# Roots as powers on GpSimd, and an adjacency scaled once, in a four-layer graph network

## The chip, the cores and the metric

The kernel runs on one core of a Trainium2 chip. The metric is the device time of one execution in microseconds (us). A core has five engines with a queue each: PE (TensorE, matrix products), DVE (VectorE), ACT (ScalarE), POOL (GpSimd) and SP (SyncE, which here only issues DMAs). Each engine takes its instructions strictly in the order in which the program holds them; an instruction whose input is late holds up everything behind it on that engine.

## The reference, cut to what matters

64 graphs of 256 nodes with 128 features, with a symmetric 0/1 adjacency each, go through four layers. Each layer adds its result to its input and normalizes every node.

```python
def _layernorm(x, eps=1e-5):
    return (x - mean(x)) / sqrt(var(x) + eps)

x = _layernorm(x + layer0(x, adj))   # max over neighbours of relu(p_i + q_j + b)
x = _layernorm(x + layer1(x, adj))   # elu products, two aggregations, tanh
x = _layernorm(x + layer2(x, adj))   # below
x = _layernorm(x + layer3(x, adj))   # sum over neighbours of gelu(layernorm(c_j + d_i)), an update, a layernorm of its own

def layer2(x, adj):
    A = adj + eye(256)
    deg = A.sum(-1)
    dinv = where(deg > 0, rsqrt(deg), 0)
    norm_A = dinv[:, None] * A * dinv[None, :]
    h = elu(elu(x @ W0 + b0))
    h = elu(norm_A @ (h @ W1) + b1)
    return norm_A @ (h @ W2) + b2
```

## The kernel before

There are two programs in the kernel. One, `sparse`, runs always; the other, `general`, stands behind a branch that is taken only if the adjacency doesn't have the expected shape, and with these inputs it is not taken. Both use the class `Shared`, which holds the layers.

In `sparse` the work of one graph is cut into four stages, each a Python generator: `first` (layer 0 and the sorting of neighbours into slots, L502), `second` (layer 1, L778), `third` (layer 2 and the start of layer 3, L782) and `last` (the rest of layer 3, L821). All 64 graphs are unrolled. At each step four graphs are in work, one in each stage (L881): `together` (L341) lets the generator that has come least far, by weights of 34, 34, 14 and 44, issue instructions up to its next `yield`. That gives an order of issue; a scheduler of the framework then makes of it the order on each engine, by readiness of the instructions and by the free buffers of the pools. So a removed instruction can also move others.

The parts that matter here:

- `inverse_root(t)` (L72) is an ACT square root in place (L74) and a DVE reciprocal in place (L75). It serves the norms (`rs`, 128x2, one column for each half of the nodes), the degrees of layer 2 (`dinv`, 128x2) and the per-message roots of layer 3 (`vr`, 128x16 or 108x16, L768).
- ACT's functions come in tables. Square root, Exp (and Tanh) and Gelu have tables of their own here, and each change between them puts a table load in front of the activation. A load carries the line of the activation behind it.
- `layernorm` (L166) takes the statistics of each half (L171, L172), writes variance plus epsilon to `rs` (L174), calls `inverse_root` between two `yield`s, and then normalizes (L180, or L184 and L185 with a gain and a shift). Each graph has five such norms: x after layers 0, 1 and 2, and z and o in `update` (L319).
- `layer_2` (L261) computes the degrees' root, adds the identity to the transposed adjacency `aT` (L277), and then twice scales the rows of `hs` by `dinv` (L293, four instructions of 128x128 per graph), multiplies by `aT` on PE (L296), copies (L299), multiplies by the weights (L304), and scales by `dinv` and adds the bias (L308).
- The degree sums `dg` are made in `first` (L544) and kept until `third`, which turns them into `deg` (L787).
- In `sums_of` and `last`, layer 3 is done in tiles of 1024 messages: PE gathers (L728), DVE adds (L732), ACT squares (L736), PE sums over the features (L743), ACT adds epsilon (L745), a trip through DRAM gives the roots a compact form (L750, L762, `vr`, L771) and spreads them over all partitions (L828), DVE multiplies (L839), ACT applies Gelu (L841), DVE adds up (L492).

Of the kernel before, what the change touches and what calls it, by code (L numbers as in the profile page):

```python
# [9 lines left out]
F32 = mybir.dt.float32  # L10
BF16 = mybir.dt.bfloat16
AF = mybir.ActivationFunctionType
ALU = mybir.AluOpType
# [6 lines left out]
P = 128  # L20
# [23 lines left out]
def kernel(  # L44
# [9 lines left out]
    nc = tc.nc  # L54
    B, N, D = x.shape
    assert N == 2 * P and D == P
    H = N // P
    Q = P // 4

    consts = ctx.enter_context(tc.tile_pool(name="consts", bufs=1))  # L60
# [8 lines left out]
    minus1 = consts.tile([P, 1], F32, name="minus1")  # L69
    nc.vector.memset(minus1, -1.0)  # L70

    def inverse_root(t):  # L72

        nc.scalar.activation(t, t, AF.Sqrt)  # L74
        nc.vector.reciprocal(t, t)  # L75

    def load(src, shape, name):
        t = consts.tile(shape, F32, name=name)
# [43 lines left out]
    with tc.tile_pool(name="prep", bufs=1) as prep, tc.tile_pool(  # L122
        name="ps_prep", bufs=2, space=bass.MemoryType.PSUM
# [33 lines left out]
    class Shared:  # L157
# [45 lines left out]
        def to_features(self, xn, name, bufs=None):  # L203
# [5 lines left out]
            nc.scalar.copy(t, pt[:, :N])  # L209
            return t  # L210

        def node_tile(self, name):
            return self.state.tile([P, H, P], F32, name=name)

# [43 lines left out]
            yield from self.layernorm(x2, y)  # L258
            s["x2"] = x2

        def layer_2(self, s, aT, deg_of):  # L261

            work, psum, elu = self.work, self.psum, self.elu
            x2 = s["x2"]
            deg = work.tile([P, H], F32, name="deg")
            deg_of(deg)
            nc.vector.tensor_scalar(deg, deg, 1.0, None, ALU.add)
            pos = work.tile([P, H], F32, name="pos")
            nc.vector.tensor_scalar(pos, deg, 0.0, None, ALU.is_gt)
            dinv = work.tile([P, H], F32, name="dinv")  # L270
            nc.vector.tensor_scalar(dinv, deg, 1e-30, None, ALU.max)
            inverse_root(dinv)
            yield
            nc.vector.tensor_mul(dinv, dinv, pos)
            for h in range(H):
                blk = aT[:, h, h * P:(h + 1) * P]
                nc.vector.tensor_add(blk, blk, ident)  # L277
            yield
            xT = self.to_features(x2, "xT_2", 1)
            yield  # L280
            ph = psum()
            hs = work.tile([P, H, P], F32, name="hs")
            for h in range(H):
                cols = slice(h * P, (h + 1) * P)
                nc.tensor.matmul(ph[:, cols], xT[:, cols], w2[0], start=True, stop=True)
            yield
            for h in range(H):
                nc.vector.tensor_add(hs[:, h], ph[:, h * P:(h + 1) * P], b2[0])
            yield from elu(hs, hs, twice=True)
            yield  # L290
            for step in (1, 2):
                for h in range(H):
                    nc.vector.tensor_scalar(hs[:, h], hs[:, h], dinv[:, h:h + 1], None, ALU.mult)  # L293
                pa = psum()
                for h in range(H):
                    nc.tensor.matmul(pa[:, :N], hs[:, h], aT[:, h], start=h == 0, stop=h == H - 1)  # L296
                yield
                agg = work.tile([P, N], F32, name="agg")
                nc.scalar.copy(agg, pa[:, :N])  # L299
                yield  # L300
                po = psum()
                for h in range(H):
                    cols = slice(h * P, (h + 1) * P)
                    nc.tensor.matmul(po[:, cols], agg[:, cols], w2[step], start=True, stop=True)  # L304
                yield
                hs = work.tile([P, H, P], F32, name="hs")
                for h in range(H):
                    nc.vector.scalar_tensor_tensor(  # L308
                        hs[:, h], po[:, h * P:(h + 1) * P], dinv[:, h:h + 1], b2[step], ALU.mult, ALU.add
                    )  # L310
                if step == 1:
                    yield from elu(hs, hs)
                yield
            nc.vector.tensor_add(hs, hs, x2)
            x3 = self.node_tile("x3")
            yield from self.layernorm(x3, hs)
            s["x3"] = x3
# [36 lines left out]
    def sparse(ctx):  # L354
# [35 lines left out]
        with tc.tile_pool(name="cs_prep", bufs=1) as pp:  # L390
            t = pp.tile([P, P], F32, name="upto_f")
# [4 lines left out]
            t = pp.tile([P, N], I32, name="iota_i")  # L396
            nc.gpsimd.iota(t, pattern=[[1, N]], base=0, channel_multiplier=0)
            nc.vector.tensor_copy(iota_k, t)
            t = pp.tile([P, 1], I32, name="part_i")
# [25 lines left out]
            t = pp.tile([P, 1], F32, name="gbe")  # L425
# [9 lines left out]
            for i in range(3):  # L435
                t = pp.tile([3, P], BF16, name="u_part")
# [5 lines left out]
            t = pp.tile([ROWS, g_n, g_w], F32, name="tail_f")  # L442
# [7 lines left out]
        state = ctx.enter_context(tc.tile_pool(name="state", bufs=2))  # L450
# [4 lines left out]
        sh = Shared(work, state, ps_mm)  # L455
# [46 lines left out]
        def first(g, s):  # L502
# [37 lines left out]
            nc.scalar.activation(diff, diff, AF.Abs, accum_out=fl[:, 0:1])  # L540
            kc = work.tile([P, H, H], F32, name="kc")
            nc.vector.scalar_tensor_tensor(kc, pc, -1.0, down_c, ALU.mult, ALU.subtract)
            dg = state.tile([P, H], F32, name="dg", bufs=3)
            nc.vector.tensor_reduce(dg, pc, AX.X, ALU.add)  # L544
            s["dg"] = dg

            more = work.tile([P, H, H], F32, name="more")
            for h in range(H):
# [169 lines left out]
        def sums_of(s, i):  # L718
# [46 lines left out]
                fu[:rows],  # L765
                s["fulls"].rearrange("h w -> (h w)")[first_at:first_at + n].rearrange("(p k) -> p k", k=PIECE),
            )
            inverse_root(vr[:rows])  # L768
            nc.vector.tensor_mul(vr[:rows], vr[:rows], fu[:rows])
            out_line = dram.tile([1, GROUP * TILE], F32, name="scale_line")  # L770
            nc.sync.dma_start(out_line[:, :n].rearrange("o (p k) -> (o p) k", k=PIECE), vr[:rows])  # L771
# [9 lines left out]

        def third(g, s):  # L782

            dg = s["dg"]

            def deg_of(deg):
                nc.vector.tensor_scalar(deg, dg, 1.0 / N, None, ALU.mult)  # L787

            yield from sh.layer_2(s, s["aT"], deg_of)
            yield  # L790
            x3, perm = s["x3"], s["perm"]

            x3T = sh.to_features(x3, "x3T")
            yield
            pc = psum()
            for h in range(H):
                nc.tensor.matmul(
                    pc[:, h * N:(h + 1) * N], x3T[:, h * P:(h + 1) * P], w3c.rearrange("p c o -> p (c o)"),
                    start=True, stop=True,
                )  # L800
            pcv = pc.rearrange("p (h c o) -> p h c o", h=H, c=2)
            dn = work.tile([P, H, P], F32, name="dn")
            nc.scalar.copy(dn, pcv[:, :, 1])
            c3 = state.tile([P, 3, H, P], BF16, name="c3")
            split3(c3, pcv[:, :, 0])
            yield
            pd = psum()
            for h in range(H):
                for hi in range(H):
                    nc.tensor.matmul(  # L810
                        pd[:, h * N:(h + 1) * N], dn[:, hi], perm[:, h, hi], start=hi == 0, stop=hi == H - 1
                    )
            yield
            dT = state.tile([P, H, N], F32, name="dT")
            nc.scalar.activation(dT, pd.rearrange("p (h n) -> p h n", h=H), AF.Identity, bias=b3c)
            s.update(x3T=x3T, c3=c3, dT=dT)
            yield
            for i in range(AHEAD):
                yield from sums_of(s, i)
# [75 lines left out]
    def general(ctx):  # L895
# [82 lines left out]
        def middle(g, s):  # L978
# [7 lines left out]
                nc.scalar.copy(aT[:, hj], pt[:, :N])  # L986
            yield

            def deg_of(deg):
                nc.vector.tensor_reduce(deg, an, AX.X, ALU.add)  # L990

            yield from sh.layer_1(s, an, aT, s["x1"])
            yield
            yield from sh.layer_2(s, aT, deg_of)
            yield

            x3T = sh.to_features(s["x3"], "x3T")
# [145 lines left out]
```

## Time and profile before

| what | value |
|---|---|
| median of 3 runs | 5735.95 us (5717.65 to 5736.4) |
| the profiled execution's own time | 5731.62 us |
| its span, first to last instruction | 5729.7 us |
| mean granted TensorE clock | 0.862 |
| table loads on ACT | 1,236, 1.283 us each |
| DMA, mean busy share of 16 engines | about 20%, 64 GB/s |

The profile describes one execution. Its page gives the busy time of each engine, the chain of work that ended last (followed back from the last instruction, at each step to what released it or to the instruction before it on its engine), and groups of instructions. A group's line reads: source line, engine, operation, output and input tiles with their shapes, number, then the busy time in us and the mean ns of one, then the idle time of the engine just before them and what ended it. A line of the waits gives who waited for whom, the total in us, how many times, and the longest. The sum of busy times can count overlapping ends twice: the next instruction on DVE starts some 0.08 us before the one ahead of it is recorded as ended.

### The profile page before, as it was taken

How to read it: one execution, taken by the hardware profiler on the slowest of the kernel's cores; microseconds unless marked ns; L12 is line 12 of the kernel's file. 1: busy time of each engine (PE TensorE's matmuls, PEld its weight loads, DVE VectorE, ACT ScalarE, POOL GpSimd, SP SyncE). 2: the span in 40 equal slices, each digit the busy share in tenths (PEclk: the TensorE clock that was granted, in tenths of full speed). 3: DMA queues.
4: the chain of work that ended last, by engine and by line, in shares of the span. 5: the costliest groups of instructions: out<-in, count | busy, mean ns of one | idle time of the engine just before them, and what ended most of it. 6: DMA issues, size and time to landing. Idle time of an engine off the chain costs nothing.

```text
span 5729.7 us, 83531 instructions
## 1 busy us (share of the span) xinstructions
PE 4529.9 (79%) x27408; PEld 2508.7 (44%) x27408; DVE 4834.4 (84%) x14654; ACT 4275.2 (75%) x6485; POOL 1.9 (0%) x10
## 2 busy tenths in 40 slices
PE   5878878878778778788788788787887887877875
PEld 2444444444444444444444444444444444444443
DVE  6788888888888888888888888888888888888876
ACT  2577777777777777777777777777777777777785
POOL 0000000000000000000000000000000000000000
PEclk8888889889889889888898898898888887888986
DMA  0122222222212221221221222122212212221222
GB/s 22 44 70 63 62 63 72 62 63 66 69 57 70 65 63 63 72 63 62 63 72 62 63 65 70 59 68 65 63 62 72 64 62 63 69 66 60 68 65 74
DMA packets 292813, 365.15 MB, mean 64 GB/s; under 512 B 151952, under 2 KB 210448, under 8 KB 292368
## 3 DMA queue, kind: packets, MB, share of 16 engines
q1 hardware_dynamic: 292368, 359.73, 20.0%
q8 instruction: 217, 3.56, 0.3%
q14 instruction: 228, 1.87, 0.1%
HBM read 345.07 MB, written 14.53 MB: 63 GB/s over the span
## 4 chain that ended last, share of the span: by engine, by line
PE 52%; DVE 29%; ACT 11%; issue 4%; DMA 3%; SPq 0%; DVEq 0%; POOL 0%; ACTq 0%
PE bigp L665 11%; PE bigp L728 8%; DVE pre L839 6%; PE mm L860 5%; DVE lanes L492 4%; PE mm L743 4%; DVE hot L629 4%; DVE pre L732 4%; DVE sums L492 3%; PE bigp L681 3%; DMA rs_s<-scale_line 2%; PE mm L870 2%; PE mm L296 2%; PE mm L699 2%; PE mm L647 2%
## 5 line engine op out<-in xcount | busy, mean ns | idle before, releaser
L665 PE MATMUL bigp<-hot,q 128*128 128x512 fp8e4 (+1 forms) x3840 | 1052.3, 371 | 66.6 <-DVE lanes L492 52.6
L728 PE MATMUL bigp<-hot,c 128*128 128x512 fp8e4 (+1 forms) x3840 | 928.8, 372 | 140.2 <-DVE pre L732 140.2
L732 DVE TENSOR_TENSOR pre<-bigp,dT 128x512 f32<-128x512 f32 (+6 forms) x1664 | 846.3, 530 | 37.8 <-PE bigp L728 33.5
L492 DVE TENSOR_TENSOR lanes<-bigp,lanes 128x512 f32<-128x512 f32 (+6 forms) x1536 | 772.7, 503 | 94.6 <-PE bigp L681 86.9
L839 DVE TENSOR_TENSOR pre<-pre,rs_s 128x1024 f32<-128x1024 f32 (+1 forms) x640 | 732.9, 1150 | 48.6 <-DMA rs_s<-scale_line 48.0
L736 ACT ACTIVATE sq<-pre 128x1024 f32<-128x1024 f32 (+1 forms) x640 | 638.5, 998 | 169.9 <-DVE pre L732 163.9
L841 ACT ACT_TABLE_LOAD x535 | 686.4, 1283 | 9.5
L492 DVE TENSOR_TENSOR sums<-pre,sums 128x1024 f32<-128x1024 f32 (+6 forms) x1024 | 628.8, 614 | 41.2 <-ACT pre L841 40.7
L745 ACT ACTIVATE row<-mm,eps_t 128x256 f32<-128x256 f32 (+1 forms) x640 | 289.6, 453 | 476.9 <-PE mm L743 476.7
L841 ACT ACTIVATE pre<-pre,be,g 128x1024 f32<-128x1024 f32 (+1 forms) x512 | 594.2, 1172 | 57.8 <-DVE pre L839 53.0
L743 PE MATMUL mm<-sq,ones 128*32 128x256 f32 (+1 forms) x5120 | 482.9, 440 | 135.2 <-ACT sq L736 135.2
L74 ACT ACT_TABLE_LOAD x445 | 570.9, 1283 | 7.5
L728 PEld LDWEIGHTS <-c 128*128 128x128 bf16 x3840 | 331.2, 98 | 550.5 <-issue 136.1
L665 PEld LDWEIGHTS <-q 128*128 128x128 bf16 x3840 | 310.8, 97 | 392.6 <-issue 112.0
L296 PE MATMUL mm<-aT,hs 128*128 128x256 f32 x512 | 232.3, 600 | 316.1 <-DVE hs L293 214.8
L629 DVE TENSOR_SCALAR hot<-rank 128x512 fp8e4<-128x512 bf16 (+5 forms) x1536 | 440.5, 348 | 0.0
L681 PEld LDWEIGHTS <-pick 42*128 42x128 bf16 x2944 | 155.8, 95 | 481.5 <-issue 474.2
L296 PEld LDWEIGHTS mm<-aT,hs 128*128 128x128 f32 x512 | 135.6, 293 | 425.8 <-issue 316.1
L860 PE MATMUL mm<-w3u,sums 128*128 128x128 f32 x2048 | 296.7, 289 | 18.4 <-DVE sums L492 16.1
L194 ACT ACT_TABLE_LOAD x221 | 283.5, 1283 | 3.9
L681 PE MATMUL bigp<-lack,pick 42*128 42x36 bf16 (+16 forms) x2944 | 285.7, 187 | 0.0
L860 PEld LDWEIGHTS mm<-w3u,sums 128*128 128x128 f32 x2048 | 254.5, 195 | 37.3 <-issue 17.6
(226 smaller groups left out, 7132.6 us busy)
## 6 DMA issues: line engine op xcount, KB each, us to landing
rs_s<-scale_line SPq DMA_DIRECT2D x512, 512.0 KB
rs_s<-scale_line SPq DMA_DIRECT2D x128, 352.0 KB
an<-in_adj SPq DMA_DIRECT2D x64, 256.0 KB
x<-in_x SPq DMA_DIRECT2D x64, 128.0 KB
line<-row SPq DMA_DIRECT2D x512, 4.0 KB
out<-o SPq DMA_DIRECT2D x64, 128.0 KB
fu<-fulls SPq DMA_DIRECT2D x192, 4.0 KB
vr<-line SPq DMA_DIRECT2D x192, 8.0 KB
```

What stands on the lines that cost most here:

```text
L74: nc.scalar.activation(t, t, AF.Sqrt)
L492: nc.vector.tensor_tensor(lanes[:, :k, :w], src[:, i:i + k], lanes[:, :k, :w], op)
L629: nc.vector.tensor_scalar(hot[:, :, at:at + w], rank[:, :, :w], s0 + i + 1.0 - FAR, None, ALU.is_equal, saturate=False)
L665: nc.tensor.matmul(pt[:, :tl], q3[:, i, h], hot[:, h, t0:t0 + tl], start=i == 0, stop=False)
L681: nc.tensor.matmul(o_, l_, r_, start=False, stop=i == len(todo) - 1)
L728: nc.tensor.matmul(pt[:, :bl], c3[:, k, h], hot[:, h, t0 + b:t0 + b + bl], start=k == 0, stop=k == 2)
L732: nc.vector.tensor_add(block(pre[:, b:], n, w, at), block(pt, n, w, at), widen(dT[:, h, :w], n))
L736: nc.scalar.activation(sq[:, :tl], pre[:, :tl], AF.Square)
L743: nc.tensor.matmul(pr[q * Q:(q + 1) * Q, :tl // 4], ones[:, :Q], v4[:, :, q], start=True, stop=True)
L839: nc.vector.tensor_mul(pre[:, :tl], pre[:, :tl], rs[:, :tl])
L841: nc.scalar.activation(msg[:, :tl], pre[:, :tl], AF.Gelu, bias=be3, scale=g3)
L860: nc.tensor.matmul(pt[:, cols], lanes[:, k, cols], w3u[:, 1], start=k == 0, stop=False)
```

## The change

`inverse_root` becomes one GpSimd instruction that raises the tile to the power of a constant tile of -0.5. The roots of `vr` keep the square root on ACT and the reciprocal on DVE, now written out at their place. The degrees' root is computed in `first`, right after the degree sums, and held for `third`; its product with `pos` goes to GpSimd too. In `layer_2` the transposed adjacency is multiplied once by `dinv` (two instructions of 128x256 per graph), and the scalings of `hs` are gone. The weights of the stages stay.

```diff
+    mhalf = consts.tile([P, 16], F32, name="mhalf")
+    nc.vector.memset(mhalf, -0.5)
...
     def inverse_root(t):
-        nc.scalar.activation(t, t, AF.Sqrt)
-        nc.vector.reciprocal(t, t)
+        nc.gpsimd.tensor_tensor(t, t, mhalf[:t.shape[0], :t.free_size()], ALU.pow)
...
+        def inverse_root_of(self, deg, bufs):
+            nc.vector.tensor_scalar(deg, deg, 1.0, None, ALU.add)
+            pos = self.work.tile([P, H], F32, name="pos")
+            nc.vector.tensor_scalar(pos, deg, 0.0, None, ALU.is_gt)
+            dinv = self.state.tile([P, H], F32, name="dinv", bufs=bufs)
+            nc.vector.tensor_scalar(dinv, deg, 1e-30, None, ALU.max)
+            inverse_root(dinv)
+            nc.gpsimd.tensor_mul(dinv, dinv, pos)
+            return dinv
...
-        def layer_2(self, s, aT, deg_of):
+        def layer_2(self, s, aT, dinv_of):
...
+            dinv = dinv_of()
+            yield
             for h in range(H):
                 blk = aT[:, h, h * P:(h + 1) * P]
                 nc.vector.tensor_add(blk, blk, ident)
+            for h in range(H):
+                nc.vector.tensor_scalar(aT[:, h], aT[:, h], dinv[:, h:h + 1], None, ALU.mult)
...
             for step in (1, 2):
-                for h in range(H):
-                    nc.vector.tensor_scalar(hs[:, h], hs[:, h], dinv[:, h:h + 1], None, ALU.mult)
                 pa = psum()
...
-            dg = state.tile([P, H], F32, name="dg", bufs=3)
+            dg = work.tile([P, H], F32, name="dg")
             nc.vector.tensor_reduce(dg, pc, AX.X, ALU.add)
-            s["dg"] = dg
+            nc.vector.tensor_scalar(dg, dg, 1.0 / N, None, ALU.mult)
+            s["dinv"] = sh.inverse_root_of(dg, 4)
...
-            inverse_root(vr[:rows])
+            nc.scalar.activation(vr[:rows], vr[:rows], AF.Sqrt)
+            nc.vector.reciprocal(vr[:rows], vr[:rows])
...
-            yield from sh.layer_2(s, s["aT"], deg_of)
+            yield from sh.layer_2(s, s["aT"], lambda: s["dinv"])
```

## The prediction

> **What bounds the kernel now.** First the engines' shares and the chain of work that ended last, both on the page:
>
> ```profile
> PE 4529.9 (79%) x27408; PEld 2508.7 (44%) x27408; DVE 4834.4 (84%) x14654; ACT 4275.2 (75%) x6485; POOL 1.9 (0%) x10
> PE 52%; DVE 29%; ACT 11%; issue 4%; DMA 3%; SPq 0%; DVEq 0%; POOL 0%; ACTq 0%
> ```
>
> No engine is full. The kernel runs a fixed order of instructions over 64 graphs, and the long PE block of L728 recurs in the chain every 86 to 88 us (2900.28, 2986.94, 3074.90). So a saving counts only where the chain passes through the engine that is relieved. Second, the groups of instructions: what the change touches.
>
> ```profile
> L841 ACT ACT_TABLE_LOAD x535 | 686.4, 1283 | 9.5
> L74 ACT ACT_TABLE_LOAD x445 | 570.9, 1283 | 7.5
> L194 ACT ACT_TABLE_LOAD x221 | 283.5, 1283 | 3.9
> ...
> L75 DVE RECIPROCAL rs<-rs 128x2 f32<-128x2 f32 x320 | 48.6, 152 | 6.8 <-ACT rs L74 6.6
> ...
> L293 DVE TENSOR_SCALAR hs<-hs,dinv 128x128 f32<-128x128 f32 x256 | 61.0, 270 | 2.2
> ```
>
> ACT spends over 1,500 us on table loads. Yet added up over the whole chain, loads of L74 are on it for at most 48 us, loads of L194 for 90 us and of L198 for 42 us. ACT has gaps (25% idle), and most loads fall into them. Third, the waits, for who is late because of a norm:
>
> ```profile
> PE mm L296 <- DVE hs L293: 214.8, 67, 8.7
> ...
> PE mm L207 <- DVE x L180: 107.8, 63, 5.2
> ```
>
> PE waits 107.8/64 = 1.7 us per graph for the first norm's output. Fourth, therefore, the chain in order of time in the middle of the run (start, length, what), where that norm lies:
>
> ```profile
> 2910.05 0.16 DVE rs L174
> 2910.21 0.59 DVE pre L732
> 2910.80 0.97 DVE pre L839
> 2911.77 0.08 issue
> 2911.85 0.68 DVE pre L732
> 2912.53 0.16 DVE vr L75
> 2912.70 0.02 DVE rs L75
> 2912.72 0.59 DVE pre L732
> 2913.31 0.08 DVE vr L769
> 2913.39 0.27 DVE x L180
> 2913.66 0.05 issue
> 2913.70 0.33 PE mm L207
> ```
>
> The variance is ready at 2910.21 and the normalized x only at 2913.39. What stands between is not the root (ACT 0.20, DVE 0.15) but other work that was put between its two halves: 3.2 us in which everything that needs x waits.
>
> **What the skill says.** The Trainium skill, *ScalarE: Activation LUTs*, section "What ACT_TABLE_LOAD costs", gives about 1283 ns for a load and as much again for a drain after it. The trace has 1283 ns on every load, but no drain: a load starts at 2910.10 and its activation at 2911.39, 1.29 later. The forecast uses 1.28 us. *SBUF — State Buffer*, section "Who interferes with whom", says that a DVE instruction with two SBUF inputs and a GpSimd instruction that reads SBUF shut each other out for a whole instruction, and that one with a single SBUF input doesn't. POOL has 10 instructions here, all in the preparation, so no row tests it. I use it to pick which DVE instruction behind a power may be held up.
>
> **The change, part by part.**
>
> *ACT.* 384 square roots go: rs 320 x 0.201 = 64 us, dinv 64 x 0.203 = 13 us. In the built order of the path that runs, table loads fall from 1,236 (as in the trace) to 956: 384 for Gelu, 319 for the vr roots that stay, 250 + 2 for exp, 1 in the preparation. That is 280 x 1.283 = 359 us. ACT is relieved by 436 us, 6.8 per graph, nearly all beside other engines' work. I credit nothing for it by itself.
>
> *DVE.* Removed: the reciprocals of rs 48.6 and of dinv 9.4, dinv times pos 6.4, the scalings of hs 61.0: 125 us. Added: 128 scalings of aT, 128x256, between the 0.290 us of L197's 128x256 and the 0.347 of L560's (a scalar per partition, like this one): 37 to 44, I take 41. Net 84 us less. The aT scalings stand where the adding of the identity stood: there (2893 to 2906) DVE is busy 10.2 of 13.0 us beside a PE at 12.9, so their 0.6 per graph is covered; without that idle time they would cost 40 us. One pair of hs scalings lies ahead of L296 on the chain: 13.8 us over the run, **0.2 per graph**. The rest of the DVE saving has other work beside it.
>
> *The degrees' root* moves two stages earlier, with its four small DVE instructions of 0.16 us. They land before L226, where DVE idles 179.7/64 = 2.8 us per graph. Its wait on POOL has nobody behind it: dinv is needed a graph or more later. No DMA moves to another place that the chain shows; SP's order changes in a few neighbours only, and the queue rows cost 0.
>
> *The order on DVE.* This is the largest term. The built order closes the gap between L174 and its user. From the end of the maximum (m L706) to x L180 the chain took 7.08 us in the graph shown and 6.10 in the next (the old order alternates between two patterns; 2992.97 to 2999.07). The new order has one pattern. Ahead of x it leaves L732 (192 wide) 0.27, L707 0.33, two o 0.53, L709 0.33, two statistics 0.39 and two aggregates 0.18, one L839 1.13, L732 0.60, rs 0.16, L732 0.60: 4.5 us, steps from start to start in this trace. Saved: 2.6 and 1.6, mean **2.1 per graph**. The L839 and L732s that stood there come after x, into DVE's 2.8 us before L226; without that idle time nothing would be gained. Next late is then ACT: a Gelu with its load (1.28 + 1.24) now precedes the signs. And one L839 (1.13) leaves the chain between exp and the permutation. I net these two at **0.3**.
>
> *What POOL adds.* 384 powers, 64 products, some 7 per graph. The unknown is the time T from L174's end to when its user may start. No POOL row shows a power. From below: the 128x1 iota, 0.13 us, plus a hand-over of about 0.02, so about 0.2. From above no row binds it. The longest POOL row takes 0.45 us[...]: I set 2.0, some four times that row. I take **0.7**. In the built order DVE has this work between L174 and the user: 0.60 for x of layer 0, 0.60 for o, 1.2 for x of layer 2, 2.0 for z, 2.2 for x of layer 1. A T above that stalls the whole DVE queue, and PE and ACT behind it. For o the second instruction (L707) has two SBUF inputs, so by the port rule the cover is only 0.27. At T = 0.7: o 0.4 and x 0.1, **0.5 per graph**. A port clash could also delay the power itself by up to one L839 (1.2), but none stands in the next place after an L174.
>
> Sum: 2.1 + 0.3 + 0.2 - 0.5 = 2.1 us per graph. With 63 steady graphs that is 130 us off the profiled execution, whose time was 5731.62 (span 5729.7): 5601. The median of the three runs, 5735.95, stands 4 us higher, so 5600 to 5606; I say **5600**.
>
> **The rivals.**
>
> 1. *The power is slow* and its wait takes the place of the table loads. Stalls on the chain are (T - 0.27) + (T - 0.6) + (T - 1.2) against a gain of 2.6: even at T = 1.55. At T = 2.0 the loss is 3.9 - 2.6 = 1.3 per graph, 84 over 63: **5815**, slower. For it: five norms per graph wait in order on DVE, two of them with only 0.6 us of cover. Against: 2 elements per partition are little work.
> 2. *Another chain takes over.* If x comes earlier but signs, permutation and the PE blocks don't, only the hs scaling and a part of the DVE saving remain: 0.2 + 0.4 per graph (84/64 us times DVE's 29% of the chain), about 40: **5690**. For it: PE is at 20.4 of 21.0 us between 2872 and 2893, and DVE at 20.1. Against: the wait of L207 for x.
> 3. *The freed ACT counts too.* In every second graph the chain runs through exp and Gelu with five loads within 12 us (3014 to 3026). If the new order takes two of them off as well, 2.6 every second graph, and T stays under 0.3: 2.6 + 1.3 = 3.9 per graph, 245: **5485**.
>
> That the change does not do what it says is excluded by the built order: the roots are on POOL, and the vr roots stay on ACT with their loads.
>
> **How the numbers follow.** The main case, 5540 to 5665 (T from 0.2 to about 1): 0.52. Rival 3, below 5540: 0.15. Rival 2, 5665 to 5765: 0.17, of which 0.10 is within 0.5%. Rival 1: 0.16. About 0.5% (29 us) is what a measurement can tell from no change. Faster: 0.52 + 0.15 + 0.07 = 0.74; same 0.10; slower 0.16. The range goes from rival 3's price to 5780, where T is about 1.8; that leaves out some 0.06 below and 0.13 above.
>
> **What would show it.** Right: 956 table loads of 1.28; a chain in which x follows its rs by about 0.8 us; no wait of DVE on POOL above 0.5 per graph; the L728 block every 85 us. The cover is wrong if DVE waits on POOL at L180 or L185 for over 100 us in all. The port step is right if L707 takes visibly longer than 0.416. The hs step is right if PE's wait at L296 shrinks. The forecast is wrong if POOL shows powers above 1.5 us, or if the recurrence of L728 stays at 87 with x early.

## The result, and the profile after

| | before | after |
|---|---|---|
| median, runs on the same chip | 5731.27 us (5717.65 to 5743.04, 6 runs) | 5767.69 us (5758.81 to 5791.5, 6 runs) |
| ratio, 95% interval | | 1.0075 [1.0048, 1.0101] |
| profiled execution, its span | 5731.62, 5729.7 | 5764.43, 5762.3 |
| mean granted TensorE clock | 0.862 | 0.837 |
| table loads on ACT | 1,236 | 956 |

The change costs 0.75%; forecast was a gain of 2.3%. In the changed kernel the line numbers of before are 2 to 13 higher: L174 is L176, L180 is L182, L226 is L239, L296 is L301, L604 is L610, L706 is L712, L728 is L734, L839 is L841.

The page of the changed kernel, engines and shares of the chain:

```profile
PE 4622.5 (80%) x27408; PEld 2579.4 (45%) x27408; DVE 4805.0 (83%) x14079; ACT 3870.4 (67%) x5821; POOL 279.0 (5%) x458
PE 51%; DVE 30%; ACT 10%; issue 4%; DMA 2%; POOL 1%; SPq 0%; POOLq 0%; DVEq 0%; ACTq 0%
```

ACT lost 405 us of work and DVE 29. (The forecast had 436 and 84. It summed the means of single instructions, and these count overlapping ends twice: on DVE 0.08 us for each of 575 instructions fewer, some 46 us.) PE has the same 27,408 instructions and took 93 us longer for them. That is the line to stop at. The groups:

```profile
L843 ACT ACT_TABLE_LOAD x384 | 492.7, 1283 | 6.8
L774 ACT ACT_TABLE_LOAD x319 | 409.3, 1283 | 72.5 <-DMA vr<-line 67.4 <-issue 0.2
L196 ACT ACT_TABLE_LOAD x250 | 320.8, 1283 | 4.4
...
L77 POOL TENSOR_TENSOR rs<-rs,mhalf 128x2 f32<-128x2 f32 x320 | 220.6, 689 | 5105.9 <-DVE rs L176 4559.9 <-DVE lanes L497 546.0
...
L284 DVE TENSOR_SCALAR aT<-aT,dinv 128x256 f32<-128x256 f32 x128 | 39.1, 307 | 0.0
```

The loads are the forecast's, a power takes 0.69 us, and the scalings of aT wait for nothing. The waits:

```profile
PE mm L301 <- DVE hs L203: 150.1, 68, 7.9
...
DVE x L182 <- POOL rs L77: 22.1, 68, 0.9
...
DVE o L182 <- POOL rs L77: 14.2, 63, 0.9
```

At x and o DVE waits 36 us in all for POOL, 0.57 per graph: 0.35 at x and 0.22 at o. The chain in order of time, one graph, from the variance on (start, length, what):

```profile
2574.93 0.09 DVE rs L176
...
2575.15 0.70 POOL rs L77
2575.85 0.03 issue
2575.88 0.04 DVE x L182
...
2576.48 1.14 DVE pre L841
2577.61 1.20 DVE pre L738 x2
...
2580.28 1.24 ACT pre L843
...
2582.53 0.47 ACT sign L557 x2
2583.00 0.94 ACT sq L742
...
2584.42 1.28 ACT L196
...
2587.01 1.28 ACT L843
...
2588.31 1.24 ACT pre L843
2589.55 0.48 ACT nzp L577
```

x now follows its variance by 0.87 us, where 3.2 us lay between them before. But from 2580.28 on the chain is on ACT: a Gelu (L843), then the signs (L557, the activations whose sums give each node its place in the sorting) with other work and loads between them. No scaling of aT and nothing of the degrees' root is on the chain of the whole run.

To see where a saving goes, I cut each graph's period at four marks in the traces: the last step of layer 0's maximum (start of L712 on DVE), the use of layer 1's input products (start of the first L239 on DVE), the slots (L610), and the second step of L301 on PE. Means of 46 graphs in the middle of the run, in us:

| stretch | before | after | change |
|---|---|---|---|
| maximum to input products | 13.40 | 11.28 | -2.12 |
| input products to slots | 7.83 | 9.79 | +1.96 |
| slots to second L301 | 13.33 | 11.58 | -1.75 |
| second L301 to next maximum (the long PE block) | 52.64 | 55.41 | +2.77 |
| period | 87.2 | 88.1 | +0.9 |

The saving of the forecast is there, in its place and at its size: from the end of the maximum to x the mean falls from 6.55 to 5.01 us, 1.5 where 2.1 less a stall of 0.5 was forecast. The two stretches behind it, on both sides of the slots, lose 0.2 together: some 1.2 us of DVE's work per graph left the second of them and stands in the first now. The PE block loses 2.8.

### The profile page after: what moved, and what is told of

The parts are those of the page before. It is cut to its first block, busy times and chain, and to the rows that moved or that the text cites. A ratio compares the mean times of both kernels' runs of the same rounds, so it can differ in the third digit from the quotient of the medians.

```text
span 5762.3 us, 82873 instructions
## 1 busy us (share of the span) xinstructions
PE 4622.5 (80%) x27408; PEld 2579.4 (45%) x27408; DVE 4805.0 (83%) x14079; ACT 3870.4 (67%) x5821; POOL 279.0 (5%) x458
## 4 chain that ended last, share of the span: by engine, by line
PE 51%; DVE 30%; ACT 10%; issue 4%; DMA 2%; POOL 1%; SPq 0%; POOLq 0%; DVEq 0%; ACTq 0%
PE bigp L671 12%; PE bigp L734 9%; DVE hot L635 7%; PE mm L862 5%; DVE pre L738 4%; DVE sums L497 3%; DVE lanes L497 3%; PE bigp L687 3%; DVE pre L841 3%; ACT pre L843 2%; PE mm L872 2%; PE mm L301 2%; PE mm L705 2%; PE mm L812 2%; PE mm L749 2%
## 5 line engine op out<-in xcount | busy, mean ns | idle before, releaser
L734 PE MATMUL bigp<-hot,c 128*128 128x512 fp8e4 (+1 forms) x3840 | 1017.3, 391 | 182.2 <-DVE pre L738 182.2
L738 DVE TENSOR_TENSOR pre<-bigp,dT 128x512 f32<-128x512 f32 (+6 forms) x1664 | 851.6, 529 | 95.2 <-PE bigp L734 93.3
L497 DVE TENSOR_TENSOR lanes<-bigp,lanes 128x512 f32<-128x512 f32 (+6 forms) x1536 | 773.9, 504 | 102.5 <-PE bigp L687 91.3
L841 DVE TENSOR_TENSOR pre<-pre,rs_s 128x1024 f32<-128x1024 f32 (+1 forms) x640 | 734.6, 1148 | 62.1 <-DMA rs_s<-scale_line 61.7
L843 ACT ACTIVATE pre<-pre,be,g 128x1024 f32<-128x1024 f32 (+1 forms) x512 | 600.6, 1174 | 93.2 <-DVE pre L841 86.3
L497 DVE TENSOR_TENSOR sums<-pre,sums 128x1024 f32<-128x1024 f32 (+6 forms) x1024 | 628.8, 614 | 16.5 <-ACT pre L843 16.0
L734 PEld LDWEIGHTS <-c 128*128 128x128 bf16 x3840 | 342.3, 102 | 637.9 <-DVE pre L738 215.7
L671 PEld LDWEIGHTS <-q 128*128 128x128 bf16 x3840 | 323.6, 100 | 344.3 <-issue 101.9
L77 POOL TENSOR_TENSOR rs<-rs,mhalf 128x2 f32<-128x2 f32 x320 | 220.6, 689 | 5105.9 <-DVE rs L176 4559.9
L301 PE MATMUL mm<-aT,hs 128*128 128x256 f32 x512 | 261.3, 665 | 150.1 <-DVE hs L203 150.1
L862 PEld LDWEIGHTS mm<-w3u,sums 128*128 128x128 f32 x2048 | 273.9, 207 | 149.6 <-DVE sums L497 118.6
L862 PE MATMUL mm<-w3u,sums 128*128 128x128 f32 x2048 | 311.0, 300 | 16.4 <-DVE sums L497 16.4
```

The source lines that it names most:

```text
L497: nc.vector.tensor_tensor(lanes[:, :k, :w], src[:, i:i + k], lanes[:, :k, :w], op)
L671: nc.tensor.matmul(pt[:, :tl], q3[:, i, h], hot[:, h, t0:t0 + tl], start=i == 0, stop=False)
L734: nc.tensor.matmul(pt[:, :bl], c3[:, k, h], hot[:, h, t0 + b:t0 + b + bl], start=k == 0, stop=k == 2)
L738: nc.vector.tensor_add(block(pre[:, b:], n, w, at), block(pt, n, w, at), widen(dT[:, h, :w], n))
L841: nc.vector.tensor_mul(pre[:, :tl], pre[:, :tl], rs[:, :tl])
L843: nc.scalar.activation(msg[:, :tl], pre[:, :tl], AF.Gelu, bias=be3, scale=g3)
```

## The experiments

Theories at the start: **A**, the order (what ACT and DVE now do ahead of the signs and the block, the Gelu above all). **B**, the wait for the power. **C**, the adjacency part. Later **D**: PE's granted clock. The table gives all runs; each was compared with the kernel before on its own chip. Loads are us per graph. "Half" is PE work per graph done at half clock, from the trace's clock records; like the period, it is the mean of 46 graphs. In the changed kernel's trace, of two 128x512 products in a row the second starts 427 ns behind the first at half clock and 216 ns at full clock (medians), so a microsecond of work at half clock is at most half a microsecond lost.

| run | edit | us | ratio [95%] | period | half | loads |
|---|---|---|---|---|---|---|
| before | | 5731 | | 87.2 | 15.6 | 25.0 |
| after | | 5768 | 1.0075 [1.0048, 1.0101] | 88.1 | 20.7 | 19.2 |
| e1_norms | norms' powers only | 5788 | 1.0110 [1.0089, 1.0132] | 87.9 | 15.3 | 21.8 |
| e2_adj | adjacency only | 5943 | 1.0377 [1.0355, 1.0398] | 90.8 | 18.6 | 23.1 |
| e8_deg | adjacency, degrees as power | 5765 | 1.0063 [1.0039, 1.0088] | 88.4 | 18.3 | 21.8 |
| e4_prod | product for power | 5653 | 0.9865 [0.9846, 0.9885] | 86.2 | 17.4 | 19.2 |
| e3_twice | power twice | 5822 | 1.0174 [1.0155, 1.0193] | 88.6 | 18.7 | 19.3 |
| e5_vr | vr as power too | 6035 | 1.0538 [1.0518, 1.0559] | 92.3 | 21.8 | 7.7 |
| e7_w32 | weights 32, 34, 14, 44 | 5818 | 1.0170 [1.0150, 1.0190] | 88.7 | 20.0 | 15.4 |
| e9_w46 | weights 34, 34, 14, 46 | 5635 | 0.9835 [0.9808, 0.9862] | 85.9 | 11.8 | 18.0 |
| f4_before46 | before, these weights | 5648 | 0.9855 [0.9824, 0.9887] | 86.0 | 13.5 | 18.0 |
| f2_third345 | weights 34, 34.5, 14, 44 | 5820 | 1.0162 [1.0137, 1.0188] | 88.75 | 20.4 | 19.3 |
| f3_last345 | weights 34.5, 34, 14, 44 | 5597 | 0.9769 [0.9743, 0.9795] | 85.33 | 15.6 | 16.7 |
| g4_before345 | before, these weights | 5800 | 1.0130 [1.0113, 1.0147] | 88.3 | 11.8 | 26.9 |
| f1_warm | 4 idle products on PE | 5782 | 1.0112 [1.0076, 1.0148] | 88.0 | 18.0 | 19.2 |
| h1_fill | 8 idle products on PE | 5636 | 0.9832 [0.9812, 0.9852] | 85.6 | 10.5 | 19.2 |
| h2_last345_fill | f3 and 4 idle products | 5824 | 1.0157 [1.0140, 1.0174] | 89.0 | 13.1 | 16.7 |
| g1_last345_twice | f3, power twice | 5623 | 0.9821 [0.9804, 0.9837] | 85.4 | 14.4 | 16.7 |
| g2_last345_prod | f3, product for power | 5539 | 0.9671 [0.9655, 0.9688] | 84.2 | 15.0 | 16.7 |
| g3_third345_prod | f2, product for power | 5912 | 1.0324 [1.0307, 1.0341] | 90.5 | 23.9 | 19.3 |

### The parts alone

e1_norms has only the norms' roots as powers:

```diff
-            inverse_root(rs)
+            nc.gpsimd.tensor_tensor(rs, rs, mhalf[:, :H], ALU.pow)
```

> Only the five norms' roots become powers on GpSimd; the degrees' root, its place and the scalings of hs stay as before. Theory A (what loses is the new order: a Gelu with its table load, 2.5 us, stands in an ACT-bound stretch ahead of the signs, and two multiplications L839 stand behind the maximum, where PE then waits and falls to half its clock): in the built order of this kernel the Gelu stands ahead of the signs in both of its patterns, so it is slower than before, 5745 to 5785. Rival B (the power's own wait on DVE loses): the same powers, the same loss, 5765. Rival C (the adjacency's part loses): 5640 to 5700, the gain that was forecast for the norms.

e2_adj has only the adjacency part, all roots on ACT and DVE. e8_deg has the adjacency part with the degrees' root as a power; in the changed kernel's `layernorm`:

```diff
-            inverse_root(rs)
+            nc.scalar.activation(rs, rs, AF.Sqrt)
+            nc.vector.reciprocal(rs, rs)
```

> Only the adjacency's part: the degrees' root computed early and aT scaled once; all roots are square roots on ACT and reciprocals on DVE as before. Theory A: the built order around Gelu, signs and L839 is that of before, so 5715 to 5750, no change beyond the 0.2 us per graph of the hs scaling. Rival B: the same, no powers here. Rival C: the loss is here, 5760 to 5790.

> The changed kernel with the roots of the norms back on ACT and DVE; only the degrees' root is a power, with its product on POOL, and the adjacency is multiplied once. This is the adjacency part without the square roots that it put among the signs (that version took 5943). Theories A and B: the adjacency part itself is nearly free, the loss of that version was its table loads; 5690 to 5740. Theory C (the scalings of aT and their wait lose by themselves): 5800 to 5945.

e1 loses 1.1%, e2 3.8%, e8 0.6%, and e1's and e8's parts together, the whole change, lose 0.75%: the parts don't add. e1 is close to where A and B had it, not C; e2 missed all three. In e2 the degrees' square root puts loads among the signs (input products to slots 11.3 us, of them 11.2 busy on ACT). Without it (e8) that stretch is back at 8.0. But e8 missed its expectation by 25 us and loses nearly what the whole change loses, so theory C is not shut out by the parts alone; only its price, 5800 and more, did not come. e8's graphs stand at 88.7 us in 35 successive periods and mostly between 86.8 and 87.4 afterwards, a first sign of what follows.

### The wait for the power

e4_prod leaves out the root and takes a product in its place, which gives wrong numbers; the order of every engine is that of the changed kernel:

```diff
-    nc.vector.memset(mhalf, -0.5)
+    nc.vector.memset(mhalf, 0.005)
...
-        nc.gpsimd.tensor_tensor(t, t, mhalf[:t.shape[0], :t.free_size()], ALU.pow)
+        nc.gpsimd.tensor_tensor(t, t, mhalf[:t.shape[0], :t.free_size()], ALU.mult)
```

> The changed kernel with each power replaced by a product with 0.005 on GpSimd, so norms and degrees are scaled wrongly; the order on ACT, PE and POOL is that of the changed kernel instruction for instruction. The wait falls from about 0.75 to 0.25 us. Theory A: ACT and PE stay the bound behind it, at most 0.4 us per graph is won: 5740 to 5768. Rival B: two waits of 0.5 us per graph on the chain and whatever they push go: 5640 to 5720.

e3_twice raises the tile to the power twice, first into a spare tile:

```diff
+        nc.gpsimd.tensor_tensor(spare, t, mhalf[:t.shape[0], :t.free_size()], ALU.pow)
         nc.gpsimd.tensor_tensor(t, t, mhalf[:t.shape[0], :t.free_size()], ALU.pow)
```

> The changed kernel, with each power done twice in a row on POOL (the first into a spare tile), so that a root takes some 1.4 us in place of 0.7. The order on the other engines is nearly the same, and all numbers stay as they are. Theory B (the wait for the power sets the pace, directly and by way of a PE that is held up more often): the slope seen with the product, 115 us for 0.5 us, holds: 5890 to 5960, against 5768 for the changed kernel. Theory A (the order alone; the wait has cover): 5768 to 5820. If only the direct stalls of DVE count (some 0.7 + 0.7 + 0.25 per graph): about 5870.

e5_vr makes vr's roots powers too (`inverse_root(vr[:rows])` in place of square root and reciprocal).

> The changed kernel with the roots of vr, 128x16, as powers too: in the built order only 381 table loads are left of 956, and 2 instead of 5 of them between the maximum m and the flags. If one column costs 0.28 us ((0.69 - 0.13)/2), a power of 16 takes about 4.6 us and the trip through DRAM is longer by 3 to 4 us. Theory A: ACT-bound stretches shrink by up to 3.8 us per graph, of which half reaches the end, unless the trip becomes the bound: 5600 to 5720; if it does, 5800 and more. Rival B: five long powers in a queue ahead of the norms' powers cost more: 5850 and up.

A product takes 0.195 us. 0.5 us less wait gave 115 us, 0.7 us more cost 55: no line through these. The traces say why. From the maximum to the input products e4 gains only 0.31 us per graph (20 us over the run); most of the rest is gained in the PE block, 1.2 us per graph, and it goes with PE's clock: 3.3 us less work at half clock, by estimate up to 1.65 us per graph or 104 us. e3 loses 1.71 us per graph there (107 us), but has 2.0 us less PE work at half clock, and keeps a loss of 55. So theory B holds for 20 to 36 us; what makes the large numbers is something that answers to it. In e5 a power of 128x16 takes 3.2 us and stands in the trip of the roots through DRAM; that this makes its loss is likely, but not tested, since its order is another as well.

### Other orders

Only the weights of the stages differ, so the scheduler builds another order. f2_third345's edit, for one:

```diff
-        STAGES = [(last, 34), (third, 34), (second, 14), (first, 44)]
+        STAGES = [(last, 34), (third, 34.5), (second, 14), (first, 44)]
```

> The changed kernel with other weights of the stages, 32, 34, 14, 44 in place of 34, 34, 14, 44: the built order then has no Gelu with a load ahead of the signs, and 773 table loads in place of 956. Theory A (the Gelu ahead of the signs took the gain back, 1.9 us per graph): 5600 to 5680, and the stretch from the input products to the slots at 7.5 to 8.0 us per graph in place of 9.8. Theory B (the wait for the powers): they stay, so 5730 to 5800.

> The changed kernel with weights of 34, 34, 14, 46: a second, different order without a Gelu ahead of the signs, with 892 table loads. Theory A: 5620 to 5700. Theory B: 5730 to 5800. If this and the other order fall apart by over 100 us, the order as a whole counts, not the one Gelu.

> The kernel before with stage weights of 34, 34, 14, 46 (905 table loads in place of 1,236), as the control of the changed kernel with these weights, which took 5635. If the weights alone make that time: 5600 to 5670. If the powers on POOL are worth something once the order is good: 5680 to 5740.

> The changed kernel with stage weights of 34, 34.5, 14, 44: 953 table loads (956 in the changed kernel), but no Gelu with its load between the x of layer 1 and the sign counts. Theory A: the stretch from the input products to the slots falls from 9.8 to about 7.6 us per graph; if nothing else moves, 5768 - 63 x 2.2 = 5630; the maximum-to-products stretch may grow, since two Gelus now stand ahead of x on ACT. Theory D: the stretch falls as well, but the sum goes by how long PE runs at half clock: below 17 us of PE work at half clock per graph the kernel is faster than the changed one, above 20 it is not.

> The changed kernel with stage weights of 34.5, 34, 14, 44: the order on ACT and DVE is that of the changed kernel from the maximum to the slots, but with 836 table loads in place of 956 (all of the 120 lie elsewhere). If ACT's loads count where they lie: up to 120 x 1.28 = 154 us less, 5615. If they lie beside other work: 5740 to 5790. The Gelu in front of the signs stays, so the stretch stays at 9.5 to 9.8.

> The kernel before with weights of 34.5, 34, 14, 44: 1,329 table loads. If the weights make the 5597 of the changed kernel with these weights: 5580 to 5640. If the order that the scheduler builds is another in each kernel and the time goes by that (its loads are 93 more than before, and two Gelus with loads stand ahead of x): 5700 to 5850.

f2 takes the Gelu away from the signs, and the stretch from input products to slots falls from 9.79 to 6.21 us: theory A is right on the place. The kernel is slower all the same (5820); its PE block takes 58.0 us in place of 55.4. e7 does the same (7.0 us in that stretch, 5818). But both orders also moved other work: in f2 3.0 us of DVE's work per graph left that stretch, and the block has 2.7 us more of it. f3 keeps the Gelu there (11.1 us) and is the fastest of the complete versions, 2.3% ahead of before. e9 was expected to be an order without the Gelu ahead of the signs; in its trace a Gelu and its load do stand between x and the signs, another Gelu among them, the stretch takes 13.4 us, and the kernel gains. So the one Gelu is not what sets the time. The order as a whole does count: the same changed kernel takes 5597 to 5820 with other weights, and e9 and e7 are 183 us apart, where e9's expectation had put the mark at 100.

Does the time go by the clock, then? e9 does 11.8 us of PE work at half clock, e7 20.0, of which 1.7 and 9.9 in the PE block. But g4 has little work at half clock and is slow, with 27 us of loads per graph; and e7 has no more of it than the changed kernel and is 50 us slower. f3 has less of it and 120 loads fewer, and is close to the 5615 that the loads alone were expected to bring; it doesn't tell the two apart. The controls on the kernel before show that e9's time comes from the weights (5635 against 5648), and that f3's does not come from the weights alone (5597 against 5800).

How long are the periods? L610 runs once per graph. Its row in the changed kernel, 11 starts in the middle of the run (durations in ns, then first and last start in us):

```profile
L610 DVE TENSOR_TENSOR fl<-mm,most x11: 162/164/165, 2236.5 to 3124.3; 128x4 f32<-128x4 f32 x11
```

The same row of f2, 48 starts:

```profile
L610 DVE TENSOR_TENSOR fl<-mm,most x48: 164/164/165, 753.4 to 4924.4; 128x4 f32<-128x4 f32 x48
```

And of f3, 51 starts:

```profile
L610 DVE TENSOR_TENSOR fl<-mm,most x51: 162/164/165, 733.1 to 4999.4; 128x4 f32<-128x4 f32 x51
```

887.8 / 10 = 88.78; 4171.0 / 47 = 88.745; 4266.3 / 50 = 85.326. The trace's clock records begin and end on a grid of 3.4133 us. 26 steps of it are 88.747, 25 are 85.333. f2 and f3 keep their number throughout; the changed kernel sits at 88.7 to 88.8 in half of its graphs, and between them runs mostly at 86.1 to 87.7. That gave theory **D**: half-clock windows on this grid decide how long the PE block takes, and a graph's period locks to the grid.

### The clock by itself

More work for PE, at the same order: apart from the added products, the traces have PE, DVE and ACT in the changed kernel's order, instruction by instruction, from shortly after the start to shortly before the end. f1_warm adds four products of 128x256, whose results nobody reads, in the idle stretch ahead of the PE block; h1_fill adds four more, behind the product with `w1_nodeT`, in the last window ahead of the block:

```diff
             nc.tensor.matmul(pn[:, :N], w1_nodeT, xT, start=True, stop=True)
+            for _ in range(4):
+                nc.tensor.matmul(pn[:, N:], w1_nodeT, xT, start=True, stop=True)
...
                     nc.tensor.matmul(pa[:, :N], hs[:, h], aT[:, h], start=h == 0, stop=h == H - 1)
+                for _ in range(2 if step == 1 else 0):
+                    nc.tensor.matmul(pa[:, N:], hs[:, 0], aT[:, 0], start=True, stop=True)
...
                     nc.tensor.matmul(po[:, cols], agg[:, cols], w2[step], start=True, stop=True)
+                for _ in range(2 if step == 1 else 0):
+                    nc.tensor.matmul(po[:, N:], agg[:, :P], agg, start=True, stop=True)
```

> The changed kernel with four more products on PE per graph, whose results nobody reads: two 128x256 products into the unused half of the bank of L301's first step, two behind the first L309. The order on ACT, and nearly that on DVE, is that of the changed kernel. PE idles there (gaps of 1.5, 1.0 and 1.9 us) and its clock stays at half for 24 us on end. Theory D (PE's clock, held down where PE is 0.6 busy, makes the long PE block behind it late, and holds the period at 26 windows of 3.41 us): with PE busier there the full clock returns before that block, some 5 us of it that ran at half take 2.6 us less, so 5600 to 5690 against 5768. Theory A (ACT and the order alone): more PE work can't help; 5768 to 5830.

> The changed kernel, weights as they are, with eight more products of 128x256 on PE per graph, whose results nobody reads: two behind L301's first step, two behind the first L309, and four behind the product with w1_nodeT (L232), in the gap ahead of L301's second step. The order on ACT is that of the changed kernel, and so is DVE's up to the long PE block. Clock theory: PE enters the block at full clock, the 5.1 us per graph of it that ran at half take 2.6 us less; 5600 to 5690 against 5768. Rival (the order alone sets the period): 5768 to 5830.

f1 missed: the full clock came back, PE finished sooner, idled longer, and lost it again in the last window before the block. h1 fills that window. One graph by stretches in the changed kernel: second L301 to the first total_m, then to the maximum, then slots to second L301, then the whole graph. (Columns: stretch, length, busy time of PE, PEld, DVE, ACT, POOL, granted clock, DMA.)

```profile
2603.01:2625.65 22.64, 22.64 (x120) 12.90 (x120) 16.90 (x52) 13.87 (x22) 0.69 (x1) 0.88 0.31 100
2625.65:2659.19 33.54, 30.68 (x210) 18.58 (x209) 28.19 (x80) 16.76 (x24) 1.38 (x2) 0.95 0.20 60
...
2591.44:2603.01 11.57, 7.14 (x34) 3.05 (x35) 11.54 (x42) 11.02 (x15) 0.00 (x0) 0.50 0.03 5
2591.44:2680.19 88.75, 72.78 (x432) 40.77 (x436) 74.57 (x219) 60.51 (x93) 4.33 (x7) 0.83 0.21 64
```

The kernel before, one graph, its first two and the whole:

```profile
2592.09:2615.96 23.87, 23.39 (x126) 12.70 (x127) 18.89 (x54) 16.36 (x24) 0.00 (x0) 0.94 0.31 95
2615.96:2644.98 29.02, 27.58 (x204) 16.64 (x202) 26.55 (x85) 18.98 (x29) 0.00 (x0) 1.00 0.23 69
...
2580.19:2665.91 85.72, 70.35 (x432) 38.77 (x436) 73.83 (x223) 65.75 (x102) 0.00 (x0) 0.88 0.22 66
```

The same stretches of h1_fill as of the changed kernel:

```profile
2550.32:2571.08 20.76, 20.14 (x120) 11.05 (x120) 16.72 (x53) 13.76 (x22) 0.69 (x1) 1.00 0.35 109
2571.08:2603.07 31.99, 29.13 (x210) 17.30 (x209) 28.23 (x81) 16.76 (x24) 1.38 (x2) 1.00 0.18 63
...
2538.72:2550.32 11.60, 9.00 (x51) 5.81 (x51) 11.56 (x42) 11.06 (x15) 0.00 (x0) 0.85 0.02 4
2538.72:2624.08 85.36, 70.59 (x448) 40.34 (x452) 74.45 (x219) 60.45 (x93) 4.33 (x7) 0.92 0.20 67
```

PE has 16 more instructions and is less busy. The stretch that holds the fillers is as long as before, 11.6 us; the block behind it, at clock 1.00 in place of 0.88 and 0.95, is 3.4 us shorter in these two graphs and 2.4 in the mean of 46. DVE and ACT have nearly the same work in each stretch. 5768 to 5636: the lost clock, as far as these products bring it back, costs the changed kernel 132 us.

Not all of that is the change's doing, since the kernel before loses clock too, and before with these products was not run. The trace's clock records give this estimate. In the PE block, work at half clock rose from 3.5 us per graph before to 7.3 after; h1_fill has 0.6. h1_fill's 6.7 us less made the block 2.4 us shorter; at this rate the change's 3.9 us more cost 1.4, and 1.9 at most, of the 2.8 by which the block grew.

The rest is not the clock. With it restored, h1_fill's block (53.0 us) is no shorter than before's (52.7), in which some clock was lost. Behind its start, PE stands idle in the block for 1.4 us per graph before and 2.9 after, and after all of it is waits for DVE: 1.6 for L497 (0.9 for L492 before) and 1.3 for L738 (none before). h1_fill has the same 1.6 and 1.3. The large products of layer 0, before and after, over the run:

```profile
L665 PE MATMUL bigp<-hot,q 128*128 128x512 fp8e4 (+1 forms) x3840 | 1052.3, 371 | 66.6 <-DVE lanes L492 52.6
L671 PE MATMUL bigp<-hot,q 128*128 128x512 fp8e4 (+1 forms) x3840 | 1062.0, 373 | 183.1 <-DVE lanes L497 96.4
```

In h1_fill this idle time is 177.9 us, so it isn't the clock's. It points to DVE's new order in the block; which part of that order makes it was not tested.

h2_last345_fill puts four of these into f3.

> The kernel with weights 34.5, 34, 14, 44 (5597, period 85.33) with four more products behind the product with w1_nodeT, ahead of L301's second step, where its PE was a quarter busy for one window and then ran the head of the block at half clock, 6.1 us per graph. Clock theory: up to 3 us less per graph; with the lock, the next whole number of windows is 24 (81.92 us, 5385), half steps are 24.5 (83.6, 5490): 5385 to 5520. Rival: 5590 to 5660.

It missed both ranges by far. The fillers changed the built order there: loads in the stretch ahead of the block rose from 2.2 to 3.9 us and the stretch from 10.0 to 14.7. It settles nothing on the clock, and shows again that a small edit can cost more by the order than by itself.

### The lock

The wait for the power made longer or shorter in the two fully locked kernels, f3 (g1, g2) and f2 (g3), by the edits of e3 and e4, at the same order:

> The kernel with weights 34.5, 34, 14, 44 (5597), with each power done twice on POOL, so that a root takes 1.4 us in place of 0.7; the order is the same. In the changed kernel this cost 55 us in all, and 1.7 us per graph (107 us) between the maximum and the products. Theory D2 (the period is locked to 25 windows, 85.33 us): the wait is taken up by the slack of the lock, 5590 to 5610; or, if it is too much for it, the lock breaks and the time rises by over 100 us towards 26 windows. Rival (the order alone): 5640 to 5705, with a period that isn't a multiple of 3.41.

> The same kernel (5597) with a product by 0.005 in place of each power on POOL, at exactly the same order, so that a root takes 0.2 us in place of 0.7; norms and degrees are wrongly scaled by it. In the changed kernel this brought 115 us. Theory D2: 5585 to 5605, period still 85.33. Rival: 5480 to 5570.

> The kernel with weights 34, 34.5, 14, 44 (5820, all graphs at 88.75), with a product by 0.005 in place of each power, at exactly the same order; norms and degrees are wrongly scaled by it. Theory D2: 5805 to 5825, period still 88.75. Rival: 5700 to 5790.

g1's time, 5623, lies between the two forecasts; its period is the lock's, 85.33 from about the 16th on. One graph of f3: second L301 to the first total_m, the maximum to the input products, and the whole graph; then the same of g1:

```profile
2534.77:2558.35 23.58, 23.58 (x123) 13.20 (x123) 18.85 (x57) 14.63 (x23) 0.69 (x1) 0.87 0.33 96
2586.42:2598.99 12.57, 9.73 (x55) 4.85 (x52) 10.07 (x31) 10.44 (x18) 2.19 (x4) 0.86 0.15 45
2524.78:2610.11 85.33, 69.31 (x432) 39.05 (x436) 74.70 (x219) 58.12 (x91) 4.33 (x7) 0.88 0.22 67
```

```profile
2548.01:2570.05 22.04, 22.04 (x123) 12.38 (x123) 18.86 (x57) 14.64 (x23) 1.38 (x2) 0.94 0.31 103
2598.11:2612.21 14.10, 10.53 (x55) 5.05 (x52) 10.07 (x30) 10.45 (x18) 3.57 (x6) 0.76 0.15 42
2538.02:2623.35 85.33, 68.58 (x432) 38.44 (x436) 74.73 (x218) 58.11 (x91) 8.46 (x13) 0.88 0.21 67
```

The longer wait costs 1.53 us in the second stretch; the PE block's head, later against the grid, then runs at 0.94 in place of 0.87 and gives 1.54 back. The period is the same to 0.01 us. (The median is 27 us longer. Of the 15 us between the two profiled executions, 13 lie in the first 14 periods, ahead of the lock.)

g2 and g3 missed: g2 came out in the range of the rival, g3 in none. g2's periods repeat as 84.7, 84.8, 83.1: three graphs in 252.6 us, which is 74 steps. g3's alternate between 92.5 and 88.4: two graphs in 180.9, 53 steps. e7's alternate as well, 87.6 and 89.9, 52 steps. So the lock isn't to whole steps per graph; halves and thirds occur. And in g3 a shorter wait made the kernel 92 us slower, with PE work at half clock up from 20.4 to 23.9 us. That periods sit on the grid, singly or in twos and threes, is measured to 0.1 us in these six kernels; which fraction an order takes, and so whether a shorter wait gains or loses, I can't derive, and it stays open. Of theory D, then, the clock's price is shown at one order, by h1_fill; that it also explains the times of the other orders is not shown.

## Why the prediction was wrong

- **Right:** 956 loads of 1.283; a power of 0.69 us, 0.80 to 0.87 us from variance to its user; the degrees' root and the scalings of aT at nothing on the chain; the maximum to x (7.1 and 6.1 us before) at 5.0 us, 4.5 and a stall of 0.5 as in the sum; PE's wait at the second product from 214.8 down to 150.1. The stalls on POOL, 0.57 per graph, are near the 0.5 of the forecast by luck: x waits 0.35 (0.1 forecast) and o 0.22 (0.4).
- **Wrong, the port step:** "the cover is only 0.27". L713 has two SBUF inputs, ran beside a power in 61 of 64 graphs, and took 0.412 to 0.426 in all of them, as before (0.416). The case exists the other way round, below.
- **Wrong, "I net these two at 0.3":** the stretch in which the Gelu precedes the signs grew by 1.96 us per graph. I saw what comes late next and gave it the price of a neighbour's saving, although the Gelu and its load, 2.5 us, stand on the engine that the stretch then waits for (ACT 9.57 of 9.79 us busy). The next stretch gave 1.75 back, so the two together lost 0.2, where 0.3 and 0.2 for the hs scaling had been forecast as a gain: 0.7 per graph too much.
- **Wrong, the sum, and this decides:** it took the PE block as unchanged. I added up stretches as if PE's instructions kept their durations, and took a saving on the chain as a saving of the period. The block grew by 2.77 us per graph, more than the 2.1 of the forecast gain. The sum had no term for PE's clock, which by the estimate above is 1.4 to 1.9 of the 2.77, and none for PE's waits for DVE inside the block, 1.5 us longer, whose cause stays open. PE's 432 instructions of a graph took 70.1 us before and 71.9 after. At the same order, h1_fill with the clock restored takes 5636; that this is 36 us from the forecast is partly luck, since it also restores clock that the kernel before had lost. My test "wrong if the recurrence of L728 stays at 87 with x early" is what came: 88.75 in half of the graphs, mostly 86 to 88 in the others.

Rival 2 (another chain takes over) was the right kind, with PE's block as that chain; its price, 40 us of gain, was not. The Trainium skill, *TensorE: Matmul & The Clock Gate*, section "Part 1: The HAM clock gate", says that PE's default is half speed, that free-running windows of 3413 ns decide, and that an idle one takes the full clock away. The traces agree, with records on a grid of 3.4133 us and, below, the full clock gone after every window with PE under 0.4 busy. The page of before showed a clock of 0.862, and I didn't ask in which stretches the rest was lost.

## What to carry to other kernels

When PE has idle stretches between dense blocks, look at the granted clock by stretch before costing a change: whatever moves work against the clock windows changes PE's durations, and that can be worth as much (132 us here) as the wait that was removed (2.1 us per graph). Try a few products that nobody reads in the window ahead of a dense block, and see that the built order stays: here eight brought 132 us at the same order, the first four of them alone brought nothing, and in another kernel they upset the order and cost 4%. When an unrolled loop's period sits on the grid of the windows, a small gain or loss may not show, or show with the wrong sign, so judge an edit at more than one order.

## What the runs showed of the hardware

**What the clock goes by.** In the traces of all kernels here (20), over the 3.4133-us windows of the clock records: every one of the 3,001 windows at full clock in which PE was under 0.4 busy was followed by one at half clock, none of the 17,359 with 0.8 or more, and 558 of 3,680 between. From half clock, none of the 4,046 windows under 0.7 busy was followed by full clock, 33 of 910 between 0.7 and 0.8, and 87% of those over 0.9. So a stretch of windows 0.6 busy mostly keeps the clock it came with: half clock always (none of these came back), full clock in 859 of 924 windows with 0.6 to 0.7. The skill's page speaks of idle and busy windows; these shares are what a partly idle PE needs.

**Who waits at the port.** A power that starts behind a DVE product with two SBUF inputs waits for its end. e7_w32 in order of time, the DVE row:

```profile
2552.76 1.22 DVE L841 TENSOR_TENSOR pre<-pre,rs_s 128x1024 f32<-128x1024 f32 x1
```

And POOL's:

```profile
2552.93 1.59 POOL L77 TENSOR_TENSOR rs<-rs,mhalf 128x2 f32<-128x2 f32 x1 [30.23 <-DVE rs L176]
```

The power ends 0.54 us after the product. Such powers take 1.5 to 1.6 us in place of 0.69, in 61 of 64 graphs. In the changed kernel POOL starts first; its row in order of time:

```profile
2571.02 0.69 POOL L77 TENSOR_TENSOR rs<-rs,mhalf 128x2 f32<-128x2 f32 x1 [4.07 <-DVE rs L176]
```

And DVE's row:

```profile
2571.11 0.42 DVE L713 TENSOR_TENSOR m<-m,own 128x256 f32<-128x256 f32 x1
```

DVE is not held. The Trainium skill, *SBUF — State Buffer*, section "Who interferes with whom", has the port go to whoever starts first, for the whole instruction. The first pair of rows agrees; the second does not, and there the measurement decides. One reading is that a power of two elements reads its input in a moment; no run here tells.
